# Last stage by channels: states added on GpSimd during the recurrence, with a run-up of ten tokens

## The chip, the cores and the metric

The kernel runs on one core of one Trainium2 chip. The metric is the device time of one execution in microseconds (us). Five engines work beside each other, each through its own queue in order: TensorE (PE, with its weight loads shown apart as PEld), VectorE (DVE), ScalarE (ACT), GpSimd (POOL) and SyncE (SP), which here only issues DMAs.

## The reference, cut to what matters

```python
# x: (4, 128, 64, 64) f32; every layer sees 4 batches, 128 channels, 4096 tokens
x = L0_conv(x)                        # attention over tokens, 64 channels in q, k, v
t = to_tokens(x)                      # (4, 4096, 128)
t = t + causal_attention(layernorm(t))
Wx = layernorm(t) @ W.T               # then normalised over all 4*4096 tokens, per channel
y[0] = 0;  y[n] = sigmoid(Wx[n] + y[n-1] @ V.T)     # V orthogonal, 4096 steps
x = from_tokens(t + y)
```

The last line is where the change lies: the states `y` of the recurrence are added to `t`, the attention's result.

## The kernel before

**Two attention layers.** For each of the 4 batches the kernel runs layer 0 (8 blocks of 512 rows, 16 items each) and then layer 1 (8 causal blocks, 2g+2 items in block g). An item is one pair of score tiles: matmuls into `s_ps`, one Exp on ACT into `p`, an add into the running sum `dsum` on DVE (L846), and two items later the matmuls into `acc`. The work after a block is cut into small tasks; each item slot runs the one that has been due longest (`waiting`, `push`, L892 to L970), or else a task that prepares the next batch.

**The tasks after a block of layer 1** are `finish1` (L698): `sums` and `first` (divide, add to `xs`, write the result to a DRAM tensor `x2` by tokens with one DMA, L716, then layernorm), `second` (turn the normed block to channels: 32x32 squares by DVE, `squares` at L637, four DMAs out to `by_c` and one back, or by PE for the very last block) and `third` (project with `W`, statistics, and copy into `xs`, L742 to L758, so that `xs` holds `Wx` by channels: partition = channel, and along a partition batch, block, step in a chunk, chunk). The very last block (`final`) has nothing beside it but its own chain.

**The last stage** (L978 to L1075). The 4096 tokens of a batch are cut into 256 chunks of 16 tokens. All chunks of a batch advance together: one step is a matmul of `V` with 128x256 states (L1031), a multiply-add on DVE from PSUM (L1033) and a sigmoid on ACT (L1036), and the four batches take turns. As the state before a chunk isn't known, each chunk is run up over the last `WARM` = 11 tokens of the chunk before it from a constant state; then its 16 tokens follow. So there are 27 steps of 4 batches. At the end the run-up's state is compared with the true last state of the chunk before (L1060 to L1074, `gap`); where the root of the summed squares over 256 chunks exceeds `TOL` = 1e-6 in any channel, the flag sends the program into `general_path`, a slow fallback.

**The result.** During the recurrence SP loads `x2` into `xr` with 8 DMAs of 1 MB (L987), one token of a chunk after the other within a partition of 128 channels. The states go to `early` and, once `Wx` is used up, into `xs`. After the recurrence `residual` (L1043) turns the states to tokens with 128 matmuls by the identity into PSUM (L1050), adds them to `xr` with 32 additions of 128x512 on DVE (L1052) and writes `out_x` by tokens with 16 DMAs of 512 KB (L1054) on SP.

**What sets the order.** A scheduler places each engine's instructions by readiness and priority, so program text is no strict order; `keep_in_program_order` pins single instructions. Tile pools hand released memory on: a tile of the last stage that lies where an earlier pool lay waits for that pool's last readers, DMAs too. DMAs of a queue are issued in order, and an instruction at the head of a queue that waits holds what is behind it.

Of the kernel before, what the change touches and what calls it, by code (L numbers as in the profile page):

```python
# [9 lines left out]
F32 = mybir.dt.float32  # L10
AF = mybir.ActivationFunctionType
ALU = mybir.AluOpType
AX = mybir.AxisListType
PSUM = bass.MemoryType.PSUM

P = 128
BLK = 512
CHUNK = 1024
LN_EPS = 1e-5
BN_EPS = 1e-5  # L20


@with_exitstack
def general_path(
# [258 lines left out]
    with tc.tile_pool(name="wx", bufs=1) as wxp, tc.tile_pool(name="fwork", bufs=3) as wk:  # L283
# [25 lines left out]
        nc.vector.tensor_tensor(shift, beta, shift, ALU.subtract)  # L309

        STEPS = BLK // B
        with tc.tile_pool(name="ys", bufs=3) as ysp, tc.tile_pool(
            name="ps_y", bufs=2, space=PSUM
        ) as ps_y, tc.tile_pool(name="ps_o", bufs=2, space=PSUM) as ps_o:

            def preload(kb):
                wn = wk.tile([P, STEPS, B], F32, tag="wn", name="wn")
                nc.vector.tensor_scalar(wn, wx[:, ts(kb, STEPS), :], scale, shift, ALU.mult, ALU.add)
                ps = ps_y.tile([P, STEPS, B], F32, tag="y", name="y_ps")
                nc.tensor.matmul(ps, lhsT=ident, rhs=wn, start=True, stop=False, skip_group_check=True)  # L320
                return ps

            nblk = N // STEPS
            prev = None
            nxt = preload(0)
            for kb in range(nblk):
# [11 lines left out]
                o = ysp.tile([P, B, STEPS], F32, tag="o", name="o")  # L338
                nc.gpsimd.tensor_tensor(o, xs[:, :, ts(kb, STEPS)], y.rearrange("p t b -> p b t"), ALU.add)
                op = ps_o.tile([P, B, P], F32, tag="o", name="oT_ps")  # L340
                for b in range(B):
                    nc.tensor.transpose(op[:, b, :], o[:, b, :], ident)
                oT = ysp.tile([P, B, P], F32, tag="oT", name="oT")
                nc.vector.tensor_copy(oT, op)
                nc.sync.dma_start(out=out[:, ts(kb, STEPS), :].rearrange("b n c -> n b c"), in_=oT)

# [3 lines left out]
def fast_path(  # L350
# [27 lines left out]
    TPB = BLK // P  # L378
    SHIFT = 32.0
    LOW, HIGH = 1e-25, 1e25  # L380
    WARM, TOL, STEPS = 11, 1e-6, 16
    NCH = N // STEPS
    CPB = BLK // STEPS
    S = nc.vector.STREAM_SQUARE_SIZE
# [8 lines left out]

    xs = xpool.tile([P, B, N], F32, name="xs")

    x2 = dram.tile([B, N, P], F32, name="x2")

    def load(engine, name, shape, *parts):
        t = const.tile(shape, F32, name=name)
# [64 lines left out]
    with tc.tile_pool(name="batch", bufs=1) as batch, tc.tile_pool(name="rows", bufs=2) as rowp, tc.tile_pool(  # L464
# [169 lines left out]
                nc.tensor.transpose(ps[:, ts(j, P)], src[:, j], ident)  # L634
            engine(dst, ps)

        def squares(src):  # L637

            sq = wk.tile([P, Q, TPB, S], F32, tag="sqT", name="sqT")
            nc.vector.transpose(out=sq.rearrange("p c j t -> p j c t"), in_=src.rearrange("p j (c r) -> p j c r", r=S))  # L640
            return sq

        def in_range(last):
# [54 lines left out]
        def finish1(b, g):  # L698
# [10 lines left out]
            def first():  # L709
                if final:  # L710

                    nc.scalar.activation(spare, agg[:, 0:1], AF.Sigmoid)
                project(1, b, g, agg, mem["own"])
                if final:
                    warm(9, agg[:, : BLK // 2])
                nc.sync.dma_start(  # L716
                    out=x2[b, ts(g, BLK)].rearrange("(j p) c -> p j c", p=P),
                    in_=xs[:, b, ts(g, BLK)].rearrange("p (j c) -> p j c", c=P),
                )
                mem["xh"] = wk.tile([P, TPB, P], F32, tag="xh2", name="xh2")  # L720
                normed(b, g, mem["xh"])

            def second():
# [9 lines left out]
                for q in range(Q):  # L733
# [2 lines left out]
                        in_=sq[ts(q, S)].rearrange("r c j t -> r c (j t)"),  # L736
                    )
                nc.sync.dma_start(out=mem["xhT"], in_=by_c.rearrange("c r q k -> (c r) (q k)"))

            def third():  # L740
                wp = misc("wx_ps")
# [25 lines left out]
            else:  # L767
                yield 1, sums
                yield 3, first
            yield 3, second  # L770
            yield 1 if final else 6 if g < 2 or g == NB - 1 else 4, third


# [202 lines left out]


    with tc.tile_pool(name="xr", bufs=1) as xrp, tc.tile_pool(name="y", bufs=2) as yp, tc.tile_pool(  # L978
        name="ps_y", bufs=1, space=PSUM
    ) as ps_y, tc.tile_pool(name="ps_r", bufs=4, space=PSUM) as ps_r:  # L980

        HALVES = NCH // P
        by_chunk = lambda t: t.rearrange("b (h q s) c -> b h q s c", q=P, s=STEPS)
        xr = xrp.tile([P, B, HALVES, STEPS, P], F32, name="xr")
        for b in range(B):
            for h in range(HALVES):
                nc.sync.dma_start(out=xr[:, b, h], in_=by_chunk(x2)[b, h])  # L987

        mv = xrp.tile([P, nc.vector.BN_AGGR_DIM], F32, name="mv")
        nc.vector.bn_aggr(mv, ends)  # L990
# [16 lines left out]
        pair = lambda t: t.rearrange("p (h q) -> p h q", q=P)  # L1007

        assert HALVES * TPB == NB
        early = xrp.tile([P, B, TPB, NCH], F32, name="early")
        late = xs.rearrange("p b (r h k q) -> p b k r h q", h=HALVES, r=TPB, q=P)

        def states(b, s):
            return pair(early[:, b, s]) if s < TPB else late[:, b, s // TPB - 1, s % TPB]

        def step(b, s):

            wx = by_step[:, b, s % STEPS]  # L1020
            if s == -1:
                y = start[:, b, 1:]
            elif s < 0:
                y = yp.tile([P, NCH], F32, tag=f"y{b}", name="y")
            else:
                y = states(b, s)
            if prev[b] is None:
                nc.scalar.activation(grid(y), wx, AF.Sigmoid, scale=scale, bias=shift_half)
            else:
                ps = ps_y.tile([P, NCH], F32, tag=f"y{b}", name="y_ps")  # L1030
                nc.tensor.matmul(ps if s < 1 else pair(ps), lhsT=vf, rhs=prev[b], start=True, stop=True)  # L1031
# [4 lines left out]
                nc.scalar.activation(y, z if s < 0 else pair(z), AF.Sigmoid, bias=shift)  # L1036
            prev[b] = start[:, b, :NCH] if s == -1 else y

        for s in range(-WARM, STEPS):
            for b in range(B):  # L1040
                step(b, s)

        def residual(b):  # L1043

            for h in range(HALVES):
                for s0 in range(0, STEPS, TPB):
                    part = slice(s0 - TPB, s0 + TPB)
                    ps = ps_r.tile([P, TPB, P], F32, tag="r", name="yT_ps")
                    for j in range(TPB):
                        nc.tensor.transpose(ps[:, j], states(b, s0 + j)[:, h], ident)  # L1050
                    t = xr[:, b, h, ds(s0, TPB)]
                    nc.vector.tensor_tensor(t, t, ps, ALU.add)  # L1052
                    if s0 % (2 * TPB):
                        nc.sync.dma_start(out=by_chunk(out)[b, h, :, part], in_=xr[:, b, h, part])  # L1054

        for b in range(B - 1):
            residual(b)


        gap = xrp.tile([P, B], F32, name="gap")  # L1060
        for b in range(B):
            ps = ps_y.tile([P, NCH], F32, tag=f"y{b}", name="gap_ps")
            nc.tensor.matmul(pair(ps), lhsT=ident, rhs=prev[b], start=True, stop=False)
            nc.tensor.matmul(ps, lhsT=minus, rhs=start[:, b, 1:], start=False, stop=True)
            sq = yp.tile([P, NCH], F32, tag=f"y{b}", name="sq")
            nc.scalar.activation(sq, ps, AF.Square, accum_out=gap[:, b : b + 1])
        count = xrp.tile([P, B + 2], F32, name="count")
        nc.vector.tensor_scalar(count[:, :B], gap, TOL * TOL, None, ALU.is_le)
        nc.vector.tensor_copy(count[:, B:], good)
        total = xrp.tile([P, 1], F32, name="total")  # L1070
        nc.vector.tensor_reduce(total, count, AX.X, ALU.add)
        tp = ps_y.tile([1, 1], F32, tag="y0", name="tp")
        nc.tensor.matmul(tp, lhsT=total, rhs=ones, start=True, stop=True)
        nc.vector.tensor_scalar(flag, tp, P * (B + 2 * B * NT) - 0.5, None, ALU.is_lt)  # L1074
        residual(B - 1)  # L1075


# [58 lines left out]
```

## Time and profile before

| | us |
|---|---|
| median of 3 runs | 2074.14 (2073.96 to 2077.06) |
| the profiled execution's own time | 2073.56 |
| its span in the trace | 2071.9 |
| PE busy in the span | 2052.6 |
| DVE busy | 1488.9 |
| ACT busy | 993.6 |
| POOL busy | 117.8 |

The profiled execution's time is 1.66 us above its span; the rest of the text counts in us from the span's start. The two attention layers fill it up to about 1982; the chain of the very last block runs from there to 1995.5, the recurrence to 2045.5, and the additions and the writing of the result to the end. The mean granted TensorE clock is 0.998 of full speed.

A row of the timeline gives start, length, engine, line, operation, tiles with their shapes and count; in brackets stands how long the engine was idle before and what released it. Neighbouring rows of one kind are merged, so the length of a merged row runs from its first start to its last end. A row of the windows gives, for a stretch, its length, each engine's busy time with the number of instructions, the granted clock, the mean busy share of the 16 DMA engines and the GB/s that they moved.

### The profile page before, as it was taken

What the parts mean: (1) busy time and instruction counts of PE and PEld (TensorE: products, weight loads), DVE (VectorE), ACT (ScalarE), POOL (GpSimd) and SP (SyncE); (2) the same over time, 40 slices, a digit from 0 to 9 for tenths busy, and PEclk for the clock granted to TensorE, in tenths of its full rate; (3) what the DMA queues carried; (4) which work ended last, traced back from release to release, by engine and by line L of the source; (5) the groups of instructions that cost most, each with busy time, mean ns of one, the idle gap of its engine ahead of it and who ended that gap; (6) DMA issues with size and microseconds to landing.
All of it is one profiled execution on the core that took longest, in us unless ns stands there. A gap on an engine that the chain in (4) does not pass through costs nothing.

```text
span 2071.9 us, 30792 instructions
## 1 busy us (share of the span) xinstructions
PE 2052.6 (99%) x11716; PEld 894.6 (43%) x11716; DVE 1488.9 (72%) x2865; ACT 993.6 (48%) x1071; POOL 117.8 (6%) x221
## 2 busy tenths in 40 slices
PE   9999999999999999999999999999999999999998
PEld 3333354444333344444333335444433334444456
DVE  4899975544889986554689997554578998655578
ACT  5666632333666643333466663323366665333365
POOL 1000010000000011000000001000000001100000
PEclk9999999999999999999999999999999999999999
DMA  3110123200110113311010012230001011201044
GB/s 113 53 20 15 22 57 76 68 16 16 57 22 13 22 32 72 78 37 24 16 53 16 19 22 57 68 75 16 16 17 17 17 22 27 51 21 26 16 168 164
DMA packets 207149, 89.03 MB, mean 43 GB/s; under 512 B 140961, under 2 KB 189601, under 8 KB 205969
## 3 DMA queue, kind: packets, MB, share of 16 engines
q1 hardware_dynamic: 205984, 86.42, 16.6%
q8 instruction: 94, 1.54, 0.3%
q14 instruction: 63, 0.51, 0.1%
q0 software_dynamic: 288, 0.39, 0.1%
q10 hardware_dynamic: 720, 0.16, 0.0%
HBM read 45.84 MB, written 36.89 MB: 40 GB/s over the span
## 4 chain that ended last, share of the span: by engine, by line
PE 82%; DVE 14%; issue 1%; ACT 1%; POOL 1%; DMA 0%; DVEq 0%; ACTq 0%; POOLq 0%
PE s_ps L815 22%; PE acc L874 22%; PE s_ps L806 14%; PE acc L866 14%; DVE dsum L846 9%; PE o_ps L605 2%; PE y_ps L1031 2%; PE r_ps L570 1%; PE wx_ps L742 1%; PE kr_ps L513 1%; ACT p L820 1%; PE v_ps L525 1%; DVE xr L1052 1%; POOL ln_rstd L458 1%; DVE xs L610 1%
## 5 line engine op out<-in xcount | busy, mean ns | idle before, releaser
L846 DVE TENSOR_TENSOR dsum<-dsum,p 128x1024 f32<-128x1024 f32 x676 | 825.2, 1221 | 394.9 <-ACT p L822 304.5
L820 ACT ACTIVATE p<-s_ps,nshift 128x1024 f32<-128x1024 f32 x512 | 571.2, 1116 | 324.3 <-PE s_ps L806 267.3
L822 ACT ACTIVATE p<-s_ps 128x1024 f32<-128x1024 f32 (+2 forms) x288 | 274.5, 953 | 605.1 <-PE s_ps L815 591.2
L866 PE MATMUL acc<-p,v 64*64 64x512 f32 x4096 | 532.2, 590 | 1.9 <-ACT half L885 1.9
L806 PE MATMUL s_ps<-swap,kr 64*64 64x512 f32 x2048 | 528.2, 592 | 2.0 <-ACT p L820 1.8
L806 PE MATMUL s_ps<-kr 64*64 64x512 f32 x2048 | 528.2, 592 | 0.3
L815 PE MATMUL s_ps<-rows,xhT 128*128 128x512 f32 (+3 forms) x1152 | 502.9, 559 | 0.0
L874 PE MATMUL acc<-p,xh 128*128 128x512 f32 (+3 forms) x1152 | 500.9, 557 | 0.0
L874 PEld LDWEIGHTS acc<-p,xh 128*128 128x128 f32 x1152 | 216.2, 190 | 244.3 <-issue 233.7
L815 PEld LDWEIGHTS s_ps<-rows,xhT 128*128 128x128 f32 x1152 | 214.1, 190 | 245.5 <-issue 209.3
L866 PEld LDWEIGHTS acc<-p,v 64*64 64x64 f32 x4096 | 155.1, 133 | 284.8 <-issue 270.4
L806 PEld LDWEIGHTS s_ps<-swap,kr 64*64 64x64 f32 x2048 | 138.4, 133 | 138.8 <-issue 123.7
L806 PEld LDWEIGHTS s_ps<-kr 64*64 64x64 f32 x2048 | 138.4, 133 | 138.0 <-issue 121.0
L458 POOL TENSOR_TENSOR ln_rstd<-ln_var,mhalf 128x4 f32<-128x4 f32 x64 | 68.8, 1075 | 1181.5 <-DVE ln_var L622 1181.5
L854 DVE TENSOR_TENSOR dsum<-dsum,p 128x256 f32<-128x256 f32 (+1 forms) x120 | 55.9, 498 | 53.4 <-POOL p L826 53.4
L610 DVE SCALAR_TENSOR_TENSOR xs<-o_ps,recs,xs 128x128 f32<-128x128 f32 x256 | 73.4, 343 | 3.7 <-PE o_ps L605 0.5
L626 DVE TENSOR_SCALAR xh<-xs,ln_mv,ln_rstd 128x128 f32<-128x128 f32 x256 | 71.4, 342 | 2.2
L826 POOL TENSOR_SCALAR_AFFINE_SELECT p<-p 128x128 f32<-128x128 f32 x128 | 38.2, 322 | 511.9 <-ACT p L822 506.2
L619 DVE BATCH_NORM_STATS2 ln_st<-xs 128x6 f32<-128x128 f32 x256 | 63.5, 269 | 0.0
L459 DVE TENSOR_TENSOR ln_z<-ln_rstd 128x4 f32<-128x4 f32 x64 | 10.4, 163 | 69.9 <-POOL ln_rstd L458 69.9
L755 ACT COPY xs<-wx_ps 128x512 f32<-128x512 f32 x31 | 18.1, 585 | 72.0 <-DVE stats L745 72.0
L844 DVE COPY dsum<-p 128x1024 f32<-128x1024 f32 x60 | 41.0, 684 | 11.7 <-ACT p L822 8.1
(138 smaller groups left out, 1023.4 us busy)
## 6 DMA issues: line engine op xcount, KB each, us to landing
xs<-in_xT SPq DMA_DIRECT2D x32, 256.0 KB, 3.0
by_r<-sqT SPq DMA_DIRECT2D x128, 64.0 KB, 2.2
xhT<-by_r SPq DMA_DIRECT2D x128, 64.0 KB, 2.0
x<-xs SPq DMA_DIRECT2D x32, 256.0 KB, 2.3
xr<-x SPq DMA_DIRECT2D x8, 1024.0 KB, 11.9
out_x<-xr SPq DMA_DIRECT2D x16, 512.0 KB, 3.5
by_c<-sqT SPq DMA_DIRECT2D x124, 64.0 KB, 1.8
xhT<-by_c SPq DMA_DIRECT2D x31, 256.0 KB, 2.7
```

Source lines behind the costliest of these rows:

```text
L458: nc.gpsimd.tensor_tensor(y, var, mhalf[:, : y.shape[-1]], ALU.pow)
L610: nc.vector.scalar_tensor_tensor(t, in0=op[:, ts(j, P)], scalar=rec[:, j : j + 1], in1=t, op0=ALU.mult, op1=ALU.add)
L619: nc.vector.bn_stats(st[:, j], xs[:, b, ds(g * BLK + j * P, P)])
L626: nc.vector.tensor_scalar(dst[:, j], xs[:, b, ds(g * BLK + j * P, P)], mv[:, j, 0:1], y[:, j : j + 1], ALU.subtract, ALU.mult)
L806: nc.tensor.matmul(ps[c * M : c * M + M, off : off + n], lhsT=bs[it.b].kr[part, h, ds(t % (NT // 2) * P + c * M, M)], rhs=rows[h], start=True,
L815: nc.tensor.matmul(ps[:, off : off + n], lhsT=lhsT, rhs=rhs, start=True, stop=True)
L820: nc.scalar.activation(it.p[:, :off], ps[:, :off], AF.Exp, bias=nshift)
L822: nc.scalar.activation(it.p[:, :off], ps[:, :off], AF.Exp, scale=float(P) ** -0.5)
L846: nc.vector.tensor_tensor(flat, flat, it.p, ALU.add)
L854: nc.vector.tensor_tensor(den[:, h, q0:], den[:, h, q0:], it.p[:, o : o + n], ALU.add)
L866: nc.tensor.matmul(bt.acc[h * M : h * M + M, r], lhsT=bt.v[part, t % (NT // 2), t // (NT // 2)], rhs=it.p[part, o : o + n], start=it.first ...
L874: nc.tensor.matmul(bt.acc[:, 0, q0:], lhsT=bt.xh[:, t], rhs=it.p[:, o : o + n], start=it.first and h == 0, stop=it.last and h == 1,)
```

## The change

The result is now formed by channels. A new task `kept`, due one slot after `second`, turns each finished block of the attention's result with DVE (32x32 squares) and writes it by four DMAs to `x2`, which lies by channels. `xr` is loaded by channels (16 DMAs of 512 KB on SP, each into 32 partitions) and the states stay where `Wx` was. Each step of 128x1024 states (4 batches) is one addition: steps 0 to 11 on GpSimd, issued as soon as a step is there, their results going out on SP; steps 12 to 14, and 15 in two halves, on DVE after the recurrence, going out on ACT's queue. A result tile comes from a pool of three. The transposes by PE, `early` and the additions from PSUM are gone. The run-up is 10 tokens in place of 11, and the check takes 2e-6 in place of 1e-6. The output array lies by channels and steps and is put in order on the host as before. (The fallback is changed to write the new layout; it isn't part of the time.)

```diff
-    WARM, TOL, STEPS = 11, 1e-6, 16
+    WARM, TOL = 10, 2e-6
...
-    x2 = dram.tile([B, N, P], F32, name="x2")
+    x2 = dram.tile([B, NB, S, Q, BLK], F32, name="x2")
...
-                nc.sync.dma_start(
-                    out=x2[b, ts(g, BLK)].rearrange("(j p) c -> p j c", p=P),
-                    in_=xs[:, b, ts(g, BLK)].rearrange("p (j c) -> p j c", c=P),
-                )
...
+            def kept():
+
+                sq = squares(xs[:, b, ts(g, BLK)].rearrange("p (j c) -> p j c", c=P), final)
+                to = x2[b, g].rearrange("r c (j q t) -> r c j q t", q=Q, t=S)
+                for q in range(Q):
+                    nc.sync.dma_start(
+                        out=to[:, :, :, q].rearrange("r c j t -> r (c j) t"),
+                        in_=sq[ts(q, S)].rearrange("r c j t -> r (c j) t"),
+                    )
...
             yield 3, second
+            yield 1, kept
             yield 1 if final else 6 if g < 2 or g == NB - 1 else 4, third
...
-        xr = xrp.tile([P, B, HALVES, STEPS, P], F32, name="xr")
+        xr = xrp.tile([P, B, NCH, STEPS], F32, name="xr")
         for b in range(B):
-            for h in range(HALVES):
-                nc.sync.dma_start(out=xr[:, b, h], in_=by_chunk(x2)[b, h])
+            for c in range(Q):
+                nc.sync.dma_start(
+                    out=xr[ts(c, S), b].rearrange("r (g k) s -> r g (k s)", g=NB),
+                    in_=x2[b, :, :, c].rearrange("g r n -> r g n"),
+                )
...
             else:
-                y = states(b, s)
+                y = wx
...
+        def add(engine, s, b0=0, n=B):
+
+            t = sums.tile([P, n, NCH], F32, tag=f"t{n}", name="sum")
+            ins = engine.tensor_tensor(
+                t.rearrange("p b (g c) -> p b g c", c=CPB),
+                by_step[:, b0 : b0 + n, s],
+                xr[:, b0 : b0 + n, :, s].rearrange("p b (g c) -> p b g c", c=CPB),
+                ALU.add,
+            )
+            tc.keep_in_program_order(ins)
+            queue = nc.sync if engine is nc.gpsimd else nc.scalar
+            tc.keep_in_program_order(queue.dma_start(out=out[b0 : b0 + n, :, s].rearrange("b c k -> c b k"), in_=t))
+
+        BY_POOL = 12
         for s in range(-WARM, STEPS):
             for b in range(B):
                 step(b, s)
...
+            if 0 <= s < BY_POOL:
+                add(nc.gpsimd, s)
+        for s in range(BY_POOL, STEPS - 2):
+            add(nc.vector, s)
...
-        nc.vector.tensor_scalar(count[:, :B], gap, TOL * TOL, None, ALU.is_le)
+        pin = tc.keep_in_program_order
+        pin(nc.vector.tensor_scalar(count[:, :B], gap, TOL * TOL, None, ALU.is_le))
...
+        add(nc.vector, STEPS - 2)
+        pin(nc.vector.tensor_scalar(flag, tp, P * (B + 2 * B * NT) - 0.5, None, ALU.is_lt))
-        residual(B - 1)
+        for b0 in range(0, B, 2):
+            add(nc.vector, STEPS - 1, b0, 2)
```

More of the change, by code (lines that the diff above doesn't have):

```diff
@@ L20 @@
 BN_EPS = 1e-5
+STEPS = 16
 @with_exitstack
@@ L311, in general_path @@
         STEPS = BLK // B
-        with tc.tile_pool(name="ys", bufs=3) as ysp, tc.tile_pool(
-            name="ps_y", bufs=2, space=PSUM
-        ) as ps_y, tc.tile_pool(name="ps_o", bufs=2, space=PSUM) as ps_o:
+        with tc.tile_pool(name="ys", bufs=3) as ysp, tc.tile_pool(name="ps_y", bufs=2, space=PSUM) as ps_y:
             def preload(kb):
@@ L337, in general_path @@
                         nxt = preload(kb + 1)
-                o = ysp.tile([P, B, STEPS], F32, tag="o", name="o")
-                nc.gpsimd.tensor_tensor(o, xs[:, :, ts(kb, STEPS)], y.rearrange("p t b -> p b t"), ALU.add)
-                op = ps_o.tile([P, B, P], F32, tag="o", name="oT_ps")
+                S = out.shape[2]
+                K = STEPS // S
+                o = ysp.tile([P, B, S, K], F32, tag="o", name="o")
+                nc.gpsimd.tensor_tensor(
+                    o,
+                    xs[:, :, ts(kb, STEPS)].rearrange("p b (k s) -> p b s k", s=S),
+                    y.rearrange("p (k s) b -> p b s k", s=S),
+                    ALU.add,
+                )
                 for b in range(B):
[L342 to L345, printed above, removed]
+                    nc.sync.dma_start(out=out[b, :, :, ts(kb, K)], in_=o[:, b])
 @with_exitstack
@@ L635, in transposed, with squares @@
             engine(dst, ps)
-        def squares(src):
+        def squares(src, last=False):
             sq = wk.tile([P, Q, TPB, S], F32, tag="sqT", name="sqT")
-            nc.vector.transpose(out=sq.rearrange("p c j t -> p j c t"), in_=src.rearrange("p j (c r) -> p j c r", r=S))
+            ins = nc.vector.transpose(
+                out=sq.rearrange("p c j t -> p j c t"), in_=src.rearrange("p j (c r) -> p j c r", r=S)
+            )
+            if last:
+                tc.keep_in_program_order(ins)
             return sq
@@ L978, in fast_path @@
     with tc.tile_pool(name="xr", bufs=1) as xrp, tc.tile_pool(name="y", bufs=2) as yp, tc.tile_pool(
[L979 to L983, printed above, removed]
-        xr = xrp.tile([P, B, HALVES, STEPS, P], F32, name="xr")
-        for b in range(B):
-            for h in range(HALVES):
-                nc.sync.dma_start(out=xr[:, b, h], in_=by_chunk(x2)[b, h])
+        name="sums", bufs=3
+    ) as sums, tc.tile_pool(name="ps_y", bufs=1, space=PSUM) as ps_y:
+        xr = xrp.tile([P, B, NCH, STEPS], F32, name="xr")
+        for b in range(B):
+            for c in range(Q):
+                nc.sync.dma_start(
+                    out=xr[ts(c, S), b].rearrange("r (g k) s -> r g (k s)", g=NB),
+                    in_=x2[b, :, :, c].rearrange("g r n -> r g n"),
+                )
         mv = xrp.tile([P, nc.vector.BN_AGGR_DIM], F32, name="mv")
@@ L1006, in fast_path @@
         grid = lambda t: t.rearrange("p (g c) -> p g c", c=CPB)
[L1007 to L1016, printed above, removed]
         def step(b, s):
@@ L1021, in step @@
             if s == -1:
-                y = start[:, b, 1:]
+                y = grid(start[:, b, 1:])
             elif s < 0:
-                y = yp.tile([P, NCH], F32, tag=f"y{b}", name="y")
+                y = grid(yp.tile([P, NCH], F32, tag=f"y{b}", name="y"))
             else:
-                y = states(b, s)
+                y = wx
             if prev[b] is None:
-                nc.scalar.activation(grid(y), wx, AF.Sigmoid, scale=scale, bias=shift_half)
+                nc.scalar.activation(y, wx, AF.Sigmoid, scale=scale, bias=shift_half)
             else:
                 ps = ps_y.tile([P, NCH], F32, tag=f"y{b}", name="y_ps")
-                nc.tensor.matmul(ps if s < 1 else pair(ps), lhsT=vf, rhs=prev[b], start=True, stop=True)
+                nc.tensor.matmul(grid(ps), lhsT=vf, rhs=prev[b], start=True, stop=True)
                 z = yp.tile([P, NCH], F32, tag=f"z{b}", name="z")
@@ L1035, in step @@
                 )
-                nc.scalar.activation(y, z if s < 0 else pair(z), AF.Sigmoid, bias=shift)
-            prev[b] = start[:, b, :NCH] if s == -1 else y
+                nc.scalar.activation(y, grid(z), AF.Sigmoid, bias=shift)
+            prev[b] = grid(start[:, b, :NCH]) if s == -1 else y
+        def add(engine, s, b0=0, n=B):
[4 more added lines that the diff above has]
+                xr[:, b0 : b0 + n, :, s].rearrange("p b (g c) -> p b g c", c=CPB),
+                ALU.add,
+            )
+            tc.keep_in_program_order(ins)
+            queue = nc.sync if engine is nc.gpsimd else nc.scalar
+            tc.keep_in_program_order(queue.dma_start(out=out[b0 : b0 + n, :, s].rearrange("b c k -> c b k"), in_=t))
+        BY_POOL = 12
         for s in range(-WARM, STEPS):
@@ L1041, in fast_path @@
                 step(b, s)
[L1043 to L1057, printed above, removed]
+            if 0 <= s < BY_POOL:
+                add(nc.gpsimd, s)
+        for s in range(BY_POOL, STEPS - 2):
+            add(nc.vector, s)
         gap = xrp.tile([P, B], F32, name="gap")
@@ L1062, in fast_path @@
             ps = ps_y.tile([P, NCH], F32, tag=f"y{b}", name="gap_ps")
-            nc.tensor.matmul(pair(ps), lhsT=ident, rhs=prev[b], start=True, stop=False)
+            nc.tensor.matmul(grid(ps), lhsT=ident, rhs=prev[b], start=True, stop=False)
             nc.tensor.matmul(ps, lhsT=minus, rhs=start[:, b, 1:], start=False, stop=True)
@@ L1067, in fast_path @@
         count = xrp.tile([P, B + 2], F32, name="count")
-        nc.vector.tensor_scalar(count[:, :B], gap, TOL * TOL, None, ALU.is_le)
+        pin = tc.keep_in_program_order
+        pin(nc.vector.tensor_scalar(count[:, :B], gap, TOL * TOL, None, ALU.is_le))
         nc.vector.tensor_copy(count[:, B:], good)
         total = xrp.tile([P, 1], F32, name="total")
-        nc.vector.tensor_reduce(total, count, AX.X, ALU.add)
+        pin(nc.vector.tensor_reduce(total, count, AX.X, ALU.add))
         tp = ps_y.tile([1, 1], F32, tag="y0", name="tp")
         nc.tensor.matmul(tp, lhsT=total, rhs=ones, start=True, stop=True)
-        nc.vector.tensor_scalar(flag, tp, P * (B + 2 * B * NT) - 0.5, None, ALU.is_lt)
-        residual(B - 1)
+        add(nc.vector, STEPS - 2)
+        pin(nc.vector.tensor_scalar(flag, tp, P * (B + 2 * B * NT) - 0.5, None, ALU.is_lt))
+        for b0 in range(0, B, 2):
+            add(nc.vector, STEPS - 1, b0, 2)
 def kernel(
@@ L1122 @@
     }
-    y = nc.dram_tensor("out_x", (b, h * w, c), F32, kind="ExternalOutput").ap()
+    y = nc.dram_tensor("out_x", (b, c, STEPS, h * w // STEPS), F32, kind="ExternalOutput").ap()
     layer0 = [ins[n] for n in ("in_x", "in_c_wqT", "in_c_wkT", "in_c_wvT", "in_c_woT")]
@@ L1134 @@
     y = np.asarray(r.results[0]["out_x"])
-    return np.ascontiguousarray(y.transpose(0, 2, 1)).reshape(b, c, h, w)
+    return np.ascontiguousarray(y.transpose(0, 1, 3, 2)).reshape(b, c, h, w)
```

## The prediction

> **What bounds the kernel now.** I read the page first: PE fills nearly the whole span and carries the chain, with DVE second.
>
> ```profile
> span 2071.9 us, 30792 instructions
> ...
> PE   9999999999999999999999999999999999999998
> ...
> PE 82%; DVE 14%; issue 1%; ACT 1%; POOL 1%; DMA 0%; DVEq 0%; ACTq 0%; POOLq 0%
> ```
>
> So before 1982 only work on PE's path counts, and the change adds none there. Next the timeline of the end, where the change lies:
>
> ```profile
> 1990.10 0.69 DVE L635 COPY xhT<-xh2T_ps 128x512 f32<-128x512 f32 x1 [0.42 <-PE xh2T_ps L634]
> 1992.01 0.70 DVE L745 BATCH_NORM_STATS2 ends<-wx_ps 128x6 f32<-128x512 f32 x1 [1.22 <-PE wx_ps L742]
> 1992.10 4.08 SPq L987 DMA_DIRECT2D xr<-x  x8
> 1995.54 1.58 ACT L1028 ACTIVATE y<-xs,shift_half,scale 128x256 f32<-128x256 f32 x3 [2.21 <-DVE shift_half L1000]
> ...
> 2039.84 5.63 ACT L1036 ACTIVATE xs<-z,shift 128x256 f32<-128x256 f32 x12
> ...
> 2060.60 3.65 DVE L1052 TENSOR_TENSOR xr<-xr,yT_ps 128x512 f32<-128x512 f32 x6
> ```
>
> The recurrence runs from 1995.54 to 2045.47 (2039.84 + 5.63), 49.93 us for 27 steps, 1.85 a step. Then DVE's additions run to 2064.25, and 7.65 us follow to the end. So 26.4 us lie behind the recurrence; they are what the change can take. The windows say what fills them (columns: stretch, length, busy time of PE, PEld, DVE, ACT, POOL, clock, DMA share, GB/s):
>
> ```profile
> 1996.00:1998.00 2.00, 1.90 (x10) 1.25 (x8) 0.95 (x3) 2.00 (x5) 0.00 (x0) 1.00 1.02 426
> 2014.00:2018.00 4.00, 4.00 (x19) 3.08 (x19) 3.85 (x9) 3.98 (x9) 0.00 (x0) 1.00 0.00 0
> 2048.00:2050.00 2.00, 2.00 (x19) 1.90 (x17) 2.00 (x4) 0.15 (x1) 0.00 (x0) 1.00 0.99 404
> 2066.00:2068.00 2.00, 0.00 (x0) 0.00 (x0) 0.00 (x0) 0.00 (x0) 0.00 (x0) 0.50 0.92 352
> 2068.00:2070.00 2.00, 0.00 (x0) 0.00 (x0) 0.00 (x0) 0.00 (x0) 0.00 (x0) 0.50 0.16 66
> ```
>
> POOL is idle, and the DMA engines rest from 2014 until 2046; then DVE and the DMA engines are full together, and the data last until about 2068.3, 3.6 us before the end. Last the DMA view, whose rows give KB and median us from issue to landing:
>
> ```profile
> by_r<-sqT SPq DMA_DIRECT2D x128, 64.0 KB, 2.2
> xr<-x SPq DMA_DIRECT2D x8, 1024.0 KB, 11.9
> out_x<-xr SPq DMA_DIRECT2D x16, 512.0 KB, 3.5
> ...
> DMA packets 192, 0.26 MB, mean 109 GB/s; under 512 B 64, under 2 KB 64, under 8 KB 192
> ...
> q1 hardware_dynamic: 192, 0.26, 39.0%
> ```
>
> The last two lines belong to the stretch 125.9 to 128.3, which holds only loads into 32 partitions: 0.26 MB in 39.0% of 2.4 us of the engines is 278 GB/s at full share, against 426/1.02 = 418 for the loads of `xr` into 128.
>
> [...]
>
> **The change part by part.**
>
> *Layers.* 31 squares of 0.71 us (row of L640) join DVE, most beside PE-bound blocks of layer 1 where DVE is half idle. Three of them (g = 7 of batches 0 to 2) fall into the next layer 0, where DVE is 80 to 93% busy and later on the chain; each costs 0 to 0.7 us. The projection moves one slot. The 124 small DMAs on SP cost 0.65 us of issue each (four of L674 take 2.6), where SP has gaps; they stand ahead of the next block's `by_c` in SP's queue, which is due slots later. I take +1.0, ends 0 and 2.
>
> *Start of the recurrence.* The last block's squares follow the copy of L635, so 1990.83 to 1991.54, inside DVE's idle 1.22 us before L745: nothing. Then four DMAs of the `by_r` kind: issues of 0.65 us, the last begins at 1993.55 and lands 2.2 later, 1995.75. In the changed program the first sigmoid waits for these four (the new `y` tiles lie on the released squares), with PE and DVE behind it. It starts at 1995.9 for 1995.54: +0.35, ends 0 and 1.5.
>
> *Recurrence.* One step less: 26 x 1.83 = 47.6 (1.815 a step before transposes were mixed in, 1.85 over all). It ends at 2043.5; step 0 is there after 11 steps, at 2016.0.
>
> *Loading.* The first addition waits for the last of 16 loads. Two are issued early, by about 1982; 14 follow the four writes, from 1994.2, data from about 1995.3. They carry 7.34 MB: at 278 GB/s 26.4 us, to 2021.7[...]: 2022.6. Ends: 2016.0 (at 418 GB/s it is done before step 0) and 2035[...]. I take 278 because it is this case's own number for such a load.
>
> *Additions on GpSimd.* I take 2.5 us each[...]. Twelve take 30.0, longer than the twelve steps beside them, so POOL ends at 2052.6. Their DMAs find idle engines.
>
> *After POOL.* The addition of step 14 needs the tile of step 11 back: issue and landing of 512 KB 3.3 (L1054 took 2.9 to 3.5), the addition 1.22 (L846's shape), the flag 0.2, two halves 0.68 each: 2058.7. Steps 12 and 13 and the comparison fit in the wait. The last 256 KB are moved 2.0 later, then the 3.6 as before: 2064.3, and with the layers' +1.0 2065.3.
>
> *Gone:* 128 transposes, 32 additions of 0.68, 16 writes in a row: all inside the 26.4 us.
>
> Sum against the profiled execution: 2065.3 - 2071.9 = -6.6 on 2073.56 is 2067.0. The median of the runs lies 0.6 above that execution, so I say 2067.5.
>
> **Rivals.**
>
> *The recurrence sets the end (0.24).* If the loads end by 2016[...], POOL keeps within a step or so of the recurrence. Then DVE's steps 12 and 13 and the four squares of `gap` (0.6 each) follow 2043.5, the count and the flag end near 2047.5, and steps 14 and 15 by 2049.6; +5.6 and +1.0 give 2056.2: 2058.5 as a median. For it: the DMA engines do 418 GB/s and POOL is idle. Against: both unknowns must lie at their low ends.
>
> *The loading comes too late (0.27, slower).* Place: the 14 loads into 32 partitions ahead of the first addition. Price: [...]the additions begin at 2035.0 and end at 2065.0, and 11.7 + 1.0 behind them give 2077.7: 2080. It decides from where the loads run under 222 GB/s with 2.5 us an addition (33.0 us of loading). Against: 278 in the trace.[...]
>
> *Between (0.17).* One unknown at its bad end, one at the good: [...]the end is 2069.6, so 2072. The gain goes into the wait.
>
> *It doesn't do what it says (0.02).* The shorter run-up fails its test, and the fallback costs far more than the stage. A sigmoid's slope is at most 1/4 and V keeps lengths, so one token less costs up to a factor 4 in the meeting, where the limit gives 2. Recomputed in float32, the largest root is 0.96e-6 for 10 tokens and 0.66e-6 for 11.
>
> **How the numbers follow.** The forecast's case, POOL's chain setting the end, early enough, has 0.30; its own range is 2062 to 2070. A change is told from none here at 0.2%, about 4 us. Faster: 0.30 + 0.24 = 0.54; same: 0.17; slower: 0.27 + 0.02 = 0.29. The range takes in the recurrence's case and the late loading: 2056.5 to 2082.
>
> **What would show it.** The step right if the first addition on POOL starts near 2023 with `xr` as the last thing it waited for, POOL's starts lie 2.5 us apart, and step 14 on DVE is released by an `out_x` DMA. The loads' GB/s between 1996 and 2022 settle the largest unknown: near 278 as taken, near 200 the late case, near 420 the recurrence's. Wrong at the front if the first sigmoid waits past 1997.5 or L1033 grows while POOL adds.

## The result and the profile after

The changed kernel takes 2090.85 us (median of 4 runs, 2088.91 to 2091.30) against 2074.06 for the kernel before, run beside it: a ratio of 1.0072, 95% interval 1.0057 to 1.0087. The forecast was 2067.5, with a range that ended at 2082.0: a faster kernel was forecast, and a slower one came, above the range. The profiled execution has a span of 2088.9, 17.0 longer than before; the prediction's own sum for this span was 2065.3, so 23.6 us have to be found.

The page of the kernel after: span, busy tenths of PE, and the shares of the chain that ended last.

```profile
span 2088.9 us, 30733 instructions
...
PE   9999999999999999999999999999999999999993
...
PE 74%; DVE 18%; issue 2%; DMA 2%; POOL 1%; ACT 1%; SPq 0%; DVEq 0%; POOLq 0%; ACTq 0%
```

PE's share of the chain fell from 82 to 74%. The transfers, at 0% before, now hold 2%, some 40 us, which the chain's list by line puts down to the loads of `xr`. DVE rose from 14 to 18%. The timeline of the end of the kernel after shows where the DMA share lies:

```profile
2000.99 20.93 SPq L997 DMA_DIRECT2D xr<-x  x14
...
2002.85 2.07 ACT L1032 ACTIVATE y<-xs,shift_half,scale 128x256 f32<-128x256 f32 x4 [2.58 <-DMA x<-sqT]
...
2021.26 29.07 ACT L1040 ACTIVATE xs<-z,shift 128x256 f32<-128x256 f32 x64
...
2040.47 33.85 POOL L1046 TENSOR_TENSOR sum<-xs,xr 128x1024 f32<-128x1024 f32 x12 [39.77 <-ACT xs L1040]
...
2071.73 6.13 DVE L1046 TENSOR_TENSOR sum<-xs,xr 128x1024 f32<-128x1024 f32 x2 [21.95 <-DMA out_x<-sum]
2078.15 1.87 DVE L1046 TENSOR_TENSOR sum<-xs,xr 128x1024 f32<-128x1024 f32 x1
2080.01 1.94 DVE L1046 TENSOR_TENSOR sum<-xs,xr 128x512 f32<-128x512 f32 x2
```

The states are there from 2021.26 on, yet POOL begins at 2040.47 and ends at 2074.32, 24 us after the recurrence (2050.3). The bracket names the states as POOL's releaser, but step 0 was then 17 us old: this is a wait for several semaphores, and the one that came last is a DMA. The windows show it (stretch, length, busy time of PE, PEld, DVE, ACT, POOL, clock, DMA share, GB/s):

```profile
2004.00:2012.00 8.00, 8.00 (x36) 5.38 (x36) 7.68 (x17) 8.00 (x18) 0.00 (x0) 1.00 1.05 207
2032.00:2036.00 4.00, 4.00 (x20) 2.60 (x19) 3.96 (x10) 4.00 (x10) 0.00 (x0) 1.00 1.05 206
2036.00:2040.00 4.00, 4.00 (x19) 2.54 (x19) 3.96 (x10) 4.00 (x10) 0.00 (x0) 1.00 0.65 123
```

The 16 engines are full (1.05) at 206 GB/s; the kernel before moved 426 at 1.02. They run out of work shortly before 2040 (share 1.03 in 2037 to 2038, 0.47 in 2038 to 2039, 0.06 in the half us after it), and POOL starts at 2040.47. The DMA view has the same in two rows (KB each, us to landing):

```profile
xr<-x SPq DMA_DIRECT2D x16, 512.0 KB, 16.7
out_x<-sum SPq DMA_DIRECT2D x12, 512.0 KB, 2.9
```

From issue to landing, the wait behind the loads ahead of it included, a load of half the size now takes 16.7 us instead of 11.9.

The sum of the prediction beside what this execution did:

| term | predicted | measured | difference |
|---|---|---|---|
| layers, to the last accumulator's copy | +1.0 | +6.9 (1982.35 to 1989.29) | +5.9 |
| first sigmoid after that | +0.35 | +0.37 | 0 |
| first addition on POOL, layers apart | 2022.6 | 2033.5 (2040.47 - 6.94) | +10.9 |
| twelve additions | 30.0 | 33.85 | +3.9 |
| POOL's end to the span's end | 11.7 | 14.6 | +2.9 |

The differences make up the 23.6 us. The 26 steps took 47.5 us (predicted 47.6), off the path as it turned out.

### The profile page after: what moved, and what is told of

Its sections match the earlier page's. It is cut to its first block, busy times and chain, and to the rows that moved or that the text cites. A ratio compares the mean times of both kernels' runs of the same rounds, so it can differ in the third digit from the quotient of the medians.

```text
span 2088.9 us, 30733 instructions
## 1 busy us (share of the span) xinstructions
PE 2037.8 (98%) x11580; PEld 878.2 (42%) x11580; DVE 1493.3 (71%) x2866; ACT 991.6 (47%) x1067; POOL 148.9 (7%) x233
## 4 chain that ended last, share of the span: by engine, by line
PE 74%; DVE 18%; issue 2%; DMA 2%; POOL 1%; ACT 1%; SPq 0%; DVEq 0%; POOLq 0%; ACTq 0%
PE s_ps L828 22%; PE acc L887 22%; DVE dsum L859 12%; PE s_ps L819 12%; PE acc L879 11%; PE o_ps L607 2%; DMA xr<-x 2%; PE r_ps L572 1%; PE kr_ps L515 1%; PE wx_ps L754 1%; DVE xs L612 1%; ACT p L833 1%; POOL ln_rstd L460 1%; DVE xh L628 1%; PE v_ps L527 1%
## 5 line engine op out<-in xcount | busy, mean ns | idle before, releaser
L460 POOL TENSOR_TENSOR ln_rstd<-ln_var,mhalf 128x4 f32<-128x4 f32 x64 | 68.7, 1074 | 1192.4 <-DVE ln_var L624 1192.4
## 6 DMA issues: line engine op xcount, KB each, us to landing
xr<-x SPq DMA_DIRECT2D x16, 512.0 KB, 16.7
```

Of the source, the lines that this page charges most:

```text
L460: nc.gpsimd.tensor_tensor(y, var, mhalf[:, : y.shape[-1]], ALU.pow)
```

## The experiments

**1. Is it the 32 partitions?** The rows in DRAM stay 2 KB; one DMA now fills 128 partitions, so that four of 2 MB take the place of sixteen of 512 KB. The part of the edit that numbers the channels anew, as the expectation has it, is left out here.

```diff
-            for c in range(Q):
-                nc.sync.dma_start(
-                    out=xr[ts(c, S), b].rearrange("r (g k) s -> r g (k s)", g=NB),
-                    in_=x2[b, :, :, c].rearrange("g r n -> r g n"),
-                )
+            nc.sync.dma_start(
+                out=xr[:, b].rearrange("p (g k) s -> p g (k s)", g=NB),
+                in_=x2[b].rearrange("g r c n -> (r c) g n"),
+            )
```

> xr is read by 4 DMAs of 2 MB that fill all 128 partitions, in place of 16 of 0.5 MB that fill 32 each; the rows of 2 KB in DRAM are the same. For this the hidden channels are numbered anew: the partition r*4+c holds channel c*32+r (the weights, gamma and beta of the second block's input are ordered so on the host, and the output is put back there). The rest of the kernel is as after the change, its late layers too. Theory [...]32 partitions take in only about 205 GB/s, with 128 it is about 400 GB/s; 8.4 MB from 2002 on are then in by 2023, the first addition on GpSimd starts at about 2023.5 instead of 2040.5, its twelve of 2.82 us end at about 2057.5, what ends last is then VectorE's additions after the end of the recurrence at 2050 or about the same as GpSimd's, and the time falls by 14 to 17 us, to 2074 to 2077. Rival 'rows': 2 KB rows or the DRAM side set the 205 GB/s, then the loading ends at 2040 as before and the time stays within 2087 to 2094. Rival 'arrival does not matter': GpSimd's additions start in time but get slower beside the recurrence's VectorE work (over 4 us each), and the time is 2080 to 2090.

Measured: 2076.99 us, 13.9 below the change, ratio to before 1.0008 (0.9999 to 1.0016). The windows of this run, the additions by engine (ns: shortest, median, longest; first and last start), and two rows of its timeline:

```profile
2004.00:2012.00 8.00, 7.00 (x24) 5.27 (x25) 4.76 (x11) 6.43 (x14) 0.00 (x0) 0.79 1.02 356
```

```profile
L1048 POOL TENSOR_TENSOR sum<-xs,xr x12: 2872/2886/2907, 2026.1 to 2057.2; 128x1024 f32<-128x1024 f32 x12
```

```profile
2057.63 5.98 DVE L1048 TENSOR_TENSOR sum<-xs,xr 128x1024 f32<-128x1024 f32 x2 [4.96 <-DMA out_x<-sum]
...
2064.13 0.38 ACT L1074 ACTIVATE sq<-gap_ps 128x256 f32<-128x256 f32 x1 [9.62 <-DVE sum L1048]
```

The rate is 356 GB/s at the same share, and POOL starts 14.4 us sooner: "rows" falls, and so does "arrival does not matter", for POOL's additions beside the recurrence take 2.89 us, and in the change, where most of them lay behind it, 2.88. The DMAs are also fewer and larger here, but the 1 MB loads of the kernel before, into 128 partitions too, had 426. The start at 2026.1 is no longer set by the loads but by step 0, as the recurrence itself began late, at 2004.35: two loads of 2 MB had been issued ahead of the last `x2` writes, for which the first sigmoid waits. Its 26 steps also took 48.9 us instead of 47.5, at a granted clock of 0.79 in their first 8 us. So the wide load takes the loss away, but it makes no gain: the interval of the ratio has 1 in it. Two smaller waits come to light. DVE idles 4.96 us for a result tile, since it draws on the same three as POOL; and ACT's squares wait 9.62, because DVE's outputs stand ahead of them in ACT's queue.

**2. Would two of the narrow loads at a time do?** The 16 loads as in the change, those of the upper 64 partitions on GpSimd's queue.

```diff
-                nc.sync.dma_start(
+                (nc.sync if c < 2 else nc.gpsimd).dma_start(
```

> The change with its 16 loads of 32 partitions each, but those of the upper 64 partitions issued on GpSimd's queue and those of the lower 64 on SP's, so that two DMAs into different partitions run at a time. Theory [...]the rate goes from 205 towards 350 to 400 GB/s, the first addition on GpSimd starts at about 2026 to 2028 and the time falls by 12 to 14 us to 2075 to 2079. Rival 'DMAs of this shape are slow, whatever runs beside them' (512 rows of 2 KB, or the DRAM side): 205 GB/s stays, 2088 to 2092. Rival 'the queues take turns': the rate stays too, since the 16 engines finish one queue's DMA before the next.

Measured: 2091.0 us (one run). Three windows, the bytes of these three stretches by queue (packets, MB, share of the 16 engines; q0 is GpSimd's queue, which moves 4.59 MB over this span and 0.39 in the change; q1 has SP's), and three rows of POOL's timeline:

```profile
1996.00:2000.00 4.00, 2.24 (x7) 1.15 (x7) 2.15 (x5) 0.59 (x1) 0.42 (x1) 1.00 1.05 204
2012.00:2018.00 6.00, 1.11 (x3) 0.93 (x4) 1.27 (x8) 1.76 (x4) 1.81 (x4) 0.50 1.06 199
2020.00:2025.00 5.00, 5.00 (x18) 3.89 (x16) 3.59 (x9) 3.40 (x9) 0.00 (x0) 0.71 1.04 283
```

```profile
q0 software_dynamic: 228, 0.82, 105.4%
...
q1 hardware_dynamic: 619, 1.19, 106.0%
...
q0 software_dynamic: 244, 0.93, 63.7%
q1 hardware_dynamic: 248, 0.48, 39.5%
```

```profile
2012.68 1.16 POOL L997 DMA_DIRECT2D xr<-x  x2 [16.27 <-DMA x<-sqT]
2013.86 0.59 POOL L460 TENSOR_TENSOR scale<-var,mhalf 128x1 f32<-128x1 f32 x1
...
2039.22 33.99 POOL L1046 TENSOR_TENSOR sum<-xs,xr 128x1024 f32<-128x1024 f32 x12 [24.71 <-ACT xs L1040]
```

For most of the time the two queues did not load together. In the first stretch all bytes are GpSimd's, in the second all are SP's, and the rate is that of the change, 204 and 199 GB/s. SP's last six loads stood behind the `x2` writes in its queue, and GpSimd's last two waited for these writes until 2012.68. Where both did load, in 2020 to 2025, they moved 283 GB/s, 37% more than the 206 of the change at the same share. So in these 5 us of one run two narrow transfers into different halves of the partitions moved more together than one alone, though less than the 350 to 400 that my theory had and less than one wide transfer (356, experiment 1); neither rival, under which the rate stays, fits this stretch.

The time of this run says nothing on the rate. The loads were in by about 2030, but POOL's first addition came at 2039.22, when step 0 was there. The recurrence had begun late, at 2016.24: the batch norm's power on POOL (L460) stood behind two loads that waited 16.27 us for `x2`, and ACT and PE waited for it. That the sum is as in the change is chance.

**3. What the layers lost.** Two suspects for the accumulators' copies coming later: the square of the last block of a batch, and the projection's slot. Without the square:

```diff
             def kept():
+                if g == NB - 1 and not final:
+                    return
```

(with block 6's `sq` written to block 7's place too). With the old slot:

```diff
-            yield 1 if final else 6 if g < 2 or g == NB - 1 else 4, third
+            yield 1 if final else 6 if g < 2 else 5 if g == NB - 1 else 4, third
```

> The change as it is, but without the transpose by squares and its four DMAs for the last block (7) of batches 0 to 2; the place that they had in the order of the work stays. Block 7's part of x2 is filled with block 6's data, so that the same amount is read back: the output of block 7 in those three batches has another residual. Theory 'VectorE is full in the next batch's first block': the layers lose time in block 0 of layer 0 of batches 1, 2 and 3 because a square of 0.7 us is added there in front of the norm's statistics; without it the accumulators' copies of blocks 0 and 1 of layer 0 come at the times of before, relative to the block ahead, and 3.5 to 6 us of the 6.9 us come back. Rival 'slot': the projection's step moved by one slot in the same block, because a step was put in ahead of it, delays the block whatever VectorE does: then less than 1 us comes back. Time 2085 to 2087.5 by the first, 2089 to 2091 by the second.

> The change as it is, with the last block's projection due 5 slots after the step ahead of it instead of 6, so that it sits in the slot that it had before the change; the squares stay. Theory 'VectorE is full': nothing comes back, the end of the layers stays at 1989 (within 1 us), time 2089 to 2092. Rival 'slot': the 1.25 to 3 us lost at the start of each of batches 1 to 3 go, the layers end at 1983 to 1986, time 2084 to 2088.

> The change with both edits of the layers together: no square and no x2 writes of the last block of batches 0 to 2 (block 6's data in its place, so those blocks' residual is another), and the last block's projection in its old slot. Each alone left 0.6 of the 1.25 us lost per batch. Theory 'two costs that add': nothing is left, the copies of the accumulators come at the times of before within 0.5 us relative to the start, but for the 0.35 us steps elsewhere (1 us together); layers end at about 1983.5, time 2084 to 2085. Rival 'one bottleneck, either edit frees what there is to free': the same 3 us stay lost as with one edit, 2086.5 to 2087.5.

The third run has both edits. Measured in one run each: 2086.89, 2087.18, 2084.87. The increase from the last block's copy of one batch to the first block's of the next, against the kernel before, is a clean measure:

| into batch | change | no square | old slot | both |
|---|---|---|---|---|
| 1 | 1.24 | 0.65 | 0.58 | -0.01 |
| 2 | 1.24 | 0.64 | 0.58 | -0.01 |
| 3 | 1.24 | 0.64 | 0.58 | -0.01 |

Each edit takes about half and the two together all: two costs that add, where I had set one theory against the other. Where they arise can be seen on DVE in the first block of batch 1's layer 0. First the change's timeline, then that with the old slot (columns as above):

```profile
531.95 0.67 DVE L642 STREAM_TRANSPOSE sqT<-xs 128x512 f32<-128x512 f32 x1
532.54 11.82 DVE L859 TENSOR_TENSOR dsum<-dsum,p 128x1024 f32<-128x1024 f32 x9
544.40 0.69 DVE L903 TENSOR_TENSOR den<-dsum 128x512 f32<-128x512 f32 x1
545.01 0.69 DVE L757 BATCH_NORM_STATS2 stats<-wx_ps 128x6 f32<-128x512 f32 x1
...
547.37 0.69 DVE L857 COPY dsum<-p 128x1024 f32<-128x1024 f32 x1 [0.34 <-ACT p L833]
548.37 1.23 DVE L859 TENSOR_TENSOR dsum<-dsum,p 128x1024 f32<-128x1024 f32 x1 [0.31 <-ACT p L833]
```

```profile
532.44 0.67 DVE L642 STREAM_TRANSPOSE sqT<-xs 128x512 f32<-128x512 f32 x1
533.03 10.49 DVE L859 TENSOR_TENSOR dsum<-dsum,p 128x1024 f32<-128x1024 f32 x8
543.44 0.69 DVE L757 BATCH_NORM_STATS2 stats<-wx_ps 128x6 f32<-128x512 f32 x1
545.80 1.23 DVE L859 TENSOR_TENSOR dsum<-dsum,p 128x1024 f32<-128x1024 f32 x1 [1.67 <-ACT p L833]
```

The square's 0.67 stands ahead of additions that follow one another without a gap, and the statistics come behind them, so nearly all of it arrives. With the later slot the statistics come after nine additions and `den` instead of after eight. ACT's copy of the projection waits for them (4.20 us in the change, to 545.73), and the next Exps (546.22) and the copy of the accumulator (548.22) come behind that copy on ACT. How this makes just the other 0.6 is not shown: DVE waits for `p` in both runs, 0.34 and 0.31 in the change and 1.67 with the old slot.

The three batches are 3.7 of the 6.94 us. Steps of 0.35 in the middle of layer 0 make up 1.4 more (with both edits 1.04 are left); I didn't trace them further. Of the rest, 1.71 are not the change's: they appear in its profile alone, between blocks 0 and 1 of batch 1. The windows there, of the change and of the run with two queues, which has the same layers:

```profile
550.00:555.00 5.00, 5.00 (x40) 1.55 (x36) 2.22 (x3) 1.65 (x3) 0.19 (x1) 0.73 0.64 199
```

```profile
550.00:555.00 5.00, 5.00 (x52) 1.79 (x48) 3.46 (x4) 2.88 (x3) 0.19 (x1) 1.00 0.50 138
```

The granted clock was 0.73 and PE did 40 matmuls instead of 52. In the three other profiles with the layers of the change (experiments 1, 2 and 4) they lost 5.0, 5.2 and 5.0 from the first block on.

**4. What the stepped read costs.** The second input read in one stretch:

```diff
-                xr[:, b0 : b0 + n, :, s].rearrange("p b (g c) -> p b g c", c=CPB),
+                xr[:, b0 : b0 + n].rearrange("p b k s -> p b (k s)")[:, :, ts(s, NCH)].rearrange("p b (g c) -> p b g c", c=CPB),
```

> The change as it is, but the second input of each addition (the residual xr) is read in one contiguous stretch per partition and batch instead of one element in 16: the same amount is read, of other tokens, so the residual in the output belongs to other tokens. Theory 'the step costs': GpSimd's addition of 128x1024 falls from 2.82[...] and VectorE's, taken where GpSimd is idle, from 1.87 to about 1.22 us; [...]the time falls by 6 to 8 us. Rival 'no cost of the step': both stay (2.82 and 1.87), the time too.

Measured: 2082.99 us (one run), 7.9 below the change. The additions of this run:

```profile
L1046 POOL TENSOR_TENSOR sum<-xs,xr x12: 2308/2327/2388, 2039.9 to 2065.3; 128x1024 f32<-128x1024 f32 x12
...
L1046 DVE TENSOR_TENSOR sum<-xs,xr x5: 670/1211/2624, 2066.0 to 2072.4; 128x1024 f32<-128x1024 f32 x3, 128x512 f32<-128x512 f32 x2
```

and of the change:

```profile
L1046 POOL TENSOR_TENSOR sum<-xs,xr x12: 2875/2875/2905, 2040.5 to 2071.5; 128x1024 f32<-128x1024 f32 x12
...
L1046 DVE TENSOR_TENSOR sum<-xs,xr x5: 1002/1874/4333, 2071.7 to 2080.9; 128x1024 f32<-128x1024 f32 x3, 128x512 f32<-128x512 f32 x2
```

The step of 16 floats costs GpSimd 0.55 us (2.33 to 2.88) and DVE 0.66 (1.21 to 1.87) per addition. Twelve on POOL are 6.2 us of the gain (33.85 against 27.7), and 1.1 come behind POOL.

**5. The shorter run-up alone,** in the kernel before.

```diff
-    WARM, TOL, STEPS = 11, 1e-6, 16
+    WARM, TOL, STEPS = 10, 2e-6, 16
```

> The kernel before with one edit: a run-up of 10 tokens and a bound of 2e-6, in place of 11 and 1e-6; nothing else of the change. Theory: one step of the recurrence is 1.83 us and lies on the path, so the time falls by 1.83 us against before, 2072.2 (ratio 0.9991), and the layers stay as before. Rival 'the loads of x2 end last': the residual's loads hide the step, no change (2074).

Measured: 2072.67 us, ratio 0.9993 (0.9985 to 1.0002): 1.5 us less by the medians, which the interval doesn't tell from nothing. In the trace DVE's part of the recurrence is 46.09 us long instead of 47.88, a step less; but this execution lost 1.69 at its start, to a clock of 0.66 in 1992 to 1996. The step is gone from the path in the trace; the size of the gain in the time is not settled by these runs.

**6. A version without the waits found,** in two steps. The first has the wide load, held behind the last `x2` writes; the old slot; nine additions on GpSimd; own result tiles for DVE, written through SP.

```diff
-            queue = nc.sync if engine is nc.gpsimd else nc.scalar
+            queue = nc.sync
...
-            t = sums.tile([P, n, NCH], F32, tag=f"t{n}", name="sum")
+            t = sums.tile([P, n, NCH], F32, tag=f"t{n}" if engine is nc.gpsimd else f"v{n}", name="sum")
...
-        BY_POOL = 12
+        BY_POOL = 9
```

> The change with the 128-partition load of the run before (channels numbered anew), held behind the last x2 writes on SP so that it does not delay them; the last block's projection in its old slot; 9 of the sixteen additions on GpSimd instead of 12; VectorE's sums in buffers of their own and written out through SP, so that VectorE waits for no buffer of GpSimd's and ScalarE's squares stand behind no DMA. Theory[...]: layers end at about 1985.5, first sigmoid 13.5 later at 1999, recurrence 47.6 to 2046.6; GpSimd starts when step 0 is there, about 2021, and is done at about 2047; VectorE's additions then meet no GpSimd, all take 1.87 us (no 4.3), seven of them 13.1 and the count's steps 0.5 to about 2061, 7 us of output behind it: span 2068, time 2070, ratio to before 0.998. Rival 'VectorE's first addition is slow for another reason': one of 4 us again, 2072. Rival 'the output sets the end': 3.5 MB from VectorE at 200 GB/s are 17.5 us, end about 2 us later, 2072.

Measured: 2072.98 us, ratio 0.9993 (0.9985 to 1.0001), span 2071.0 instead of 2068. All additions of this run:

```profile
L1051 POOL TENSOR_TENSOR sum<-xs,xr x9: 2872/2896/4567, 2024.1 to 2046.8; 128x1024 f32<-128x1024 f32 x9
L1051 DVE TENSOR_TENSOR sum<-xs,xr x8: 1003/1874/4529, 2046.1 to 2062.6; 128x1024 f32<-128x1024 f32 x6, 128x512 f32<-128x512 f32 x2
```

POOL's last two and DVE's first two of these, from narrower stretches:

```profile
L1051 POOL TENSOR_TENSOR sum<-xs,xr x2: 2912/3740/4567, 2043.9 to 2046.8; 128x1024 f32<-128x1024 f32 x2
L1051 DVE TENSOR_TENSOR sum<-xs,xr x2: 2529/3529/4529, 2046.1 to 2048.5; 128x1024 f32<-128x1024 f32 x2
```

The start was right (first sigmoid at 1999.25), but the loads, all of them behind the writes now, ended at about 2023, POOL began at 2024.1 instead of 2021, and its last two additions met DVE's first two, from 2046.1. One addition of each engine then took over 4.5 us, and DVE's first took 2.53. The starts and lengths fit engines that take turns: each addition ends about its own time alone (1.87 on DVE, 2.88 on POOL) after the end of the other engine's.

| addition from | the other's ends | its own time later | it ends |
|---|---|---|---|
| 2046.1, DVE | 2046.8 | 2048.7 | 2048.6 |
| 2046.8, POOL | 2048.6 | 2051.5 | 2051.3 |
| 2048.5, DVE | 2051.3 | 2053.2 | 2053.1 |

So batch 0's load goes early again, alone, and each engine gets five result tiles:

```diff
-        for b in range(B):
+        for b in (1, 2, 3, 0):
             ins = nc.sync.dma_start(
...
-            tc.keep_in_program_order(ins)
+            if b:
+                tc.keep_in_program_order(ins)
```

> The run before with the 128-partition load and nine additions on GpSimd, with two edits: batch 0's load of 2 MB goes ahead of the last x2 writes again (the other three stay behind them), and VectorE has five buffers for its sums instead of three. Theory 'GpSimd was not done when VectorE came': there the loads ended at about 2022 and GpSimd began at 2024.1, so its last two additions met VectorE's (4.5 us each in place of 2.9 and 1.9). With 2 MB in early the loads end at about 2018, GpSimd begins when step 0 is there at about 2020.5 and ends at 2046.5, VectorE's seven are then 1.87 us each from 2046 and end at about 2060, span 2067.5, time 2069.5, ratio 0.998. Rival 'the early load delays the x2 writes and with them the first sigmoid', as with two early loads: the recurrence starts 1.5 us later and GpSimd with it, span 2069. Rival 'the output sets the end': last DMA lands at 2070 to 2071 whatever VectorE does.

Measured: 2069.61 us (median of 15 runs), ratio to before 0.9978 (0.9970 to 0.9986). The additions:

```profile
L1052 POOL TENSOR_TENSOR sum<-xs,xr x9: 2868/2892/2910, 2023.0 to 2045.6; 128x1024 f32<-128x1024 f32 x9
```

```profile
2049.44 9.11 DVE L1052 TENSOR_TENSOR sum<-xs,xr 128x1024 f32<-128x1024 f32 x5
```

POOL is done at 2048.5 before DVE begins at 2049.44, and nothing is stretched: five additions in 9.11 us. (This execution lost some 2 us in the recurrence, 49.6 for 47.5, at a granted clock of 0.66 in 2000 to 2004, so that its span of 2069.8 lies above the expected 2067.5; the median of the runs is as expected.) The last run moves the square to a later slot:

```diff
-            yield 1, kept
-            yield 1 if final else 6 if g < 2 else 5 if g == NB - 1 else 4, third
+            late = g == NB - 1 and not final
+            yield 3 if late else 1, kept
+            yield 1 if final else 6 if g < 2 else 3 if late else 4, third
```

> The same, with the square of the last block of batches 0 to 2 due three slots after the step ahead of it instead of one, and the projection three after that, in the slot it had before. Theory 'VectorE has no room in the slot where the square sits': three slots on it may have, then the 0.6 us that the square still costs in each of batches 1 to 3 go, layers 1.8 us shorter than in the run beside it, time 2067.7. Rival 'VectorE has no room anywhere in that block': no change against the run beside it, within 0.5 us.

Measured: 2069.38 us, ratio 0.9976 (0.9966 to 0.9986), no difference to the run beside it; the loss into each batch is still 0.58 to 0.59. The rival is right as far as this slot goes: the square costs the same there.

## Why the prediction was wrong, by its steps

- *What bounds, and what the change can take.* The reading of the 26.4 us behind the recurrence was right; with the waits gone they fell to 19.8 (experiment 6, 2050.06 to 2069.8). "Before 1982 only work on PE's path counts, and the change adds none there" was not: tasks on DVE, which had 14% of the chain in the line quoted, added time in layer 0 (see the layers).
- *Loading: the step that failed.* "I take 278 because it is this case's own number for such a load." The number was taken from 0.26 MB in 2.4 us at 39% share, and scaled up to a full one. Under load the change's transfers of 512 KB into 32 partitions gave 206. The 14 loads of 7.34 MB take 35.6 us at 206, against 26.4 as put in; with their slow beginning and end POOL's wait was 10.9 longer. The prediction read no load into 32 partitions with the engines full, and the late end of the loading, 2035, was an estimate that no trace showed. Experiment 1 shows that these 10.9 us, with what they covered, were the price of the 32 partitions. Why the burst ran faster stays open. Its four loads go into four different groups of 32 partitions, were issued within 1.7 us and took 2.0 each to landing, so some were under way together; 278 is close to the 283 that experiment 2 shows where two such groups were loaded at once. Loading is the largest of four terms set too low, but less than half of the miss: without its 10.9 the span would be about 2078 (estimate, 2088.9 - 10.9), still above the 2071.9 of before. The layers, the additions and what follows POOL are the others.
- *The rival "the loading comes too late"* (0.27) named the right place and side: the loads ran at 206 GB/s, under the 222 from which it decides. Its 2080 starts from the estimate of 2035 and is short, since it left the other terms at their forecast values.
- *Layers.* "Each costs 0 to 0.7 us" for the three squares was right at its upper end, about 0.6. "The projection moves one slot" got no price and cost as much again, and the 0.35 steps weren't foreseen: 5.1 in all, against +1.0 and an upper end of 2; with the 1.7 lost to the clock this makes 6.8 of the +6.9 in the table. The cover that I named, DVE "half idle" in layer 1, held; these tasks ran in the next batch's layer 0.
- *Start of the recurrence and its pace.* Right: +0.37, waiting for the four writes, and 47.5 us. L1037 took 481 ns where it had taken 480, and 480 with POOL adding from 2026.1 to the end of the recurrence (experiment 1). That POOL would leave this pace alone was an estimate: no trace of before had the two side by side.
- *Additions on GpSimd.* 2.82 between starts for the 2.5 taken, an estimate that no trace showed: 3.9 us. Without the step an addition takes 2.33 (experiment 4); the step is 0.55 of its 2.88.
- *After POOL.* 14.6 for 11.7. The wait for a tile was seen, but it hits step 12 first, whose addition then took 4.33 beside POOL's last; step 14 began 3.8 behind POOL for 3.3. DVE's durations came from an addition read without a step (1.22 for 1.87, 0.68 for 1.00): 1.0 more, as the flag's 0.2 fell beside an addition. And 6.95 from the last addition to the end, for 5.6.
- *"The recurrence sets the end"* and *"It doesn't do what it says"* did not come about.

Most of what the change loses, it loses because its load is written for 32 partitions: with the wide load the ratio to before falls from 1.0072 to 1.0008. The layers, the longer additions and the wait for tiles take the gain that was forecast. GpSimd's additions beside the recurrence left its multiply-add on DVE as long as before (480 ns in experiment 1). With the wide load, the old slot, tiles of their own and the count set so that GpSimd ends before DVE begins, the same idea, the shorter run-up included, is 0.2% faster than before.

## What to carry to other kernels

A rate scaled up from a short, sparse burst isn't a rate under load: here 278 GB/s became 206. Measure the load itself in the shape that it will have, and try a transfer that spans all partitions (356 here against 206 into 32). Give a side engine only as many additions as it ends before the main engine starts on its own, with tiles of its own: where the two met here, an addition of 2.9 us and one of 1.9 took over 4.5 each, and shared tiles held DVE for 4.96 us (experiment 1). And a task that is moved by one slot can have a price of its own, here about 0.6 us into each batch.

## What the runs showed of the hardware

- An addition with both inputs in SBUF that began on one of GpSimd and DVE while the other was in such an addition ended about its own time after the other's end. In the change DVE's began at 2071.73, POOL's last ended at 2074.32, and 1.87 after that is 2076.2; it took 4.33 us, to 2076.06, while POOL's kept its 2.88. The four in a row of experiment 6 fit the same, in both directions. Where nothing overlapped, as in the second version of experiment 6, those of 128x1024 took 2.87 to 2.91 on GpSimd and up to 1.92 on DVE.
- The loads of `xr` ran at 206 GB/s into 32 partitions at a time, at 283 where two queues loaded different halves at once (5 us of one run), and at 356 into 128 (experiment 1). The DMA engines' share was 1.02 to 1.05 each time, so a full share did not tell the rate.
- A DVE addition of 128x1024 floats with one input in steps of 64 bytes took 1.87 us against 1.21 read straight, 0.66 more; on GpSimd it took 2.88 against 2.33, 0.55 more.
- TensorE's granted clock dropped for some microseconds in single executions (0.73 in 550 to 555 of the change, 0.66 in 1992 to 1996 of experiment 5, 0.66 in 2000 to 2004 of the second version of experiment 6), beside a loss of 1.7, 1.7 and 2.1 us. What starts it stays open: PE had been as busy in the stretch before (2.65 of 5 us) in a run without the drop. A difference of 2 us between two single profiles of this kernel is worth such a look before it is explained.
